# A two-layer vision block: ScalarE's column pieces issued in twos and written in strides, small sums moved to VectorE, other pacing

## The chip, the core and the metric

The kernel runs on one core of a Trainium2 chip. The time is the device time of one execution in microseconds. Three executions of the kernel before took 2607.11, 2608.24 and 2595.48 us; the median is 2607.11. The engines are called TensorE (PE in the profile), VectorE (DVE), ScalarE (ACT), GpSimd (POOL) and SyncE (SP, which here only issues DMAs). All arithmetic is float32.

## What is computed

The input is x, 2 images of 56 x 56 positions with 384 channels. Layer 0 is neighborhood attention and an MLP, layer 1 a convolution with running averages in four directions and an MLP. The part that matters here is layer 1:

```python
h = layernorm(x)
p = h @ w_in + b_in                      # 384 -> 768 channels
local = conv3x3_depthwise(p, k_conv)
lr, rl = ema(local, axis=2), ema(local, axis=2, reverse=True)   # along rows
tb, bt = ema(local, axis=1), ema(local, axis=1, reverse=True)   # along columns
mixed = 0.25 * (lr + rl + tb + bt) + local
x = x + (layernorm(mixed) @ w_out + b_out)
out = x + gelu(layernorm(x) @ w1 + b1) @ w2 + b2
```

with ema: y[t] = 0.6 y[t-1] + 0.4 x[t].

## The kernel before

**Order of the work.** The attention fills the first quarter of the span. Then `passes` runs two loops over groups of up to 512 tokens (four tiles of 128). The first loop (`groups`) does layer 0's MLP for a group and, one group behind, layer 1's input projection `project_in`, which writes p to DRAM. The second loop (`dgroups`) does layer 1's output projection `project_out` and its MLP. In some groups at the start and in the tail of the second loop the matrix products are computed with seven half-size products in place of eight (`hidden_by_seven`, `tokens_by_seven`); they need sums of weight blocks (`sums_of_w1`, `sums_of_w2`) and of input halves (`sums_of_input`, tile `xsums`), made beforehand by GpSimd.

**Work beside TensorE.** The convolution and the scans are VectorE work with channels on the partitions. They are cut into jobs of class `Band` (some rows of one image, one block of 128 channels: eight tap instructions, two row scans) and `Columns` (one image, one block of 128 channels: the two column scans). There are six channel blocks and two images, so 12 `Columns` jobs. Class `Beside` holds the jobs and issues their instructions step by step between the matrix products: each `beside.go(worth)` adds `rate * worth` us to a debt and issues steps until their estimated times have paid it. `MLP`, `OUT` and `ROW` are such worths, 2.6, 3.9 and 7.8. `later(issue, steps)` puts something off by so many steps. `until(name)` issues everything up to a job at once. The order so found is written into the queues of the engines; each engine works through its own queue in order.

**Columns.** A scan along columns needs the image with columns laid out one after another. `turn` (L1342) makes two tiles `line`, one for each half of the columns, from two tiles `loc` (upper and lower rows): four copies of 128 x 392 for each, so eight for a job. `both_ways` (L1245) scans a tile forward and backward, 3.41 us each on VectorE. For image 0 the results go into `mixed` by VectorE (L1386). For image 1 `turn_back` (L1360) makes ScalarE write them into two tiles `mixed`, eight pieces a job (L1366), and `add_to_mix` (L1323) lets a GpSimd DMA accumulate these into `mix_d` in DRAM. The first four copies of a job are issued at the end of the job in front of it (`behind.turn`, L1318 and L1394), the other four at the first step of the job's own first scan (L1376). All copies in the run of the trace were ScalarE's. The copies read 14 columns of 28 rows: the inner loop of the read runs down a column, with a step of 56 elements, and the write is in a row.

**Buffers.** `loc` and a band's input `pt` share two buffers, `line` and a band's `loc` three, `mixed`, `both` and others four. ScalarE also empties TensorE's banks: `hid` (L1206, a hidden tile through gelu, needed every 2.58 us), `mx` (L1501), `hT` (L272, transposed input), the output copies L1882 and L1953, and the seeds L1223, which put a residual into a bank ahead of a token product. Three banks serve the hidden tiles, two the token products.

**Normalization.** In the first loop, `ahead_of` (L1758) normalizes the finished group's tokens in MLP steps 4 to 7 (tile `xn`, L255), stores them at step 8, and transposes them at step 11.

Of the kernel before, what the change touches and what calls it, by code (L numbers as in the profile page):

```python
# [35 lines left out]
ALU = mybir.AluOpType  # L36
# [30 lines left out]
HALF = H // 2  # L67
QUARTER = 14
# [45 lines left out]
class Beside:  # L114
# [3 lines left out]
    def __init__(self):  # L118
        self.jobs, self.due, self.finished, self.idle = [], 0.0, set(), True
        self.late, self.rate = [], 1.0  # L120
        self.steps = self.run()
# [55 lines left out]
def block_kernel(ctx: ExitStack, tc: tile.TileContext, ins: dict, out: bass.AP):  # L177
    nc = tc.nc
# [913 lines left out]
    def passes(xs, xn, w1, w2, between=lambda ps: None):  # L1092
# [164 lines left out]
        class Band:  # L1257
# [31 lines left out]
            def steps(self):  # L1289
                beside.behind(Band)  # L1290
                if self.loc is None:
                    self.centre(nc.vector)
                    yield us(self.n)
                loc, pt = self.loc, self.pt
                for dy in (-1, 0, 1):
                    for dx in (-1, 0, 1):
                        if dy == 0 and dx == 0:
                            continue
                        lo, hi = max(self.lo, -dy), min(self.hi, H - max(0, dy))
                        xs, xt, n = max(0, -dx), max(0, dx), W - abs(dx)  # L1300
# [12 lines left out]
                behind = beside.behind()  # L1313
                yield from both_ways(both, loc)
                if isinstance(behind, Band):
                    behind.centre()
                if isinstance(behind, Columns):
                    behind.turn(nc.scalar.copy)  # L1318
                beside.later(lambda: nc.scalar.mul(flat(both), flat(both), share), 8)  # L1319
                beside.later(lambda: add_to_mix(self.b, self.m, at, both), 11)  # L1320
# [4 lines left out]
        class Columns:  # L1325
# [15 lines left out]

            def turn(self, copy):  # L1342
                c, t = len(self.lines), half("line", "work", 3)
                for i in range(0, HALF, QUARTER):
                    for h in range(2):
                        at = slice(c * HALF + i, c * HALF + i + QUARTER)
                        copy(  # L1347
                            t[:, i : i + QUARTER, h * HALF : (h + 1) * HALF],
                            self.loc[h][:, :, at].rearrange("p h w -> p w h"),
                        )  # L1350
                self.lines.append(t)

            def steps(self):
                if not self.lines:

                    self.turn(nc.gpsimd.tensor_copy)
                    yield 2.5
                mixed, behind = [], None

                def turn_back(c):  # L1360
                    if not mixed:
                        mixed.extend(half("mixed", "out", 4) for h in range(2))
                    for i in range(0, HALF, QUARTER):
                        at = slice(c * HALF + i, c * HALF + i + QUARTER)
                        for h in range(2):
                            nc.scalar.mul(  # L1366
                                mixed[h][:, :, at],
                                self.lines[c][:, i : i + QUARTER, h * HALF : (h + 1) * HALF]
                                .rearrange("p w h -> p h w"), share,
                            )  # L1370

                for c in range(2):
                    t = self.lines[c]
                    for step, took in enumerate(both_ways(t, t)):
                        if c == 0 and step == 0:
                            self.turn(nc.scalar.copy)  # L1376
                            for h in range(2) if self.b == 0 else ():
                                mixed.append(half("mixed", "out", 4))
                                nc.sync.dma_start(out=flat(mixed[h]), in_=self.rows(mix_d, h))
                        yield took  # L1380
                        if step == 0:
                            behind = beside.behind()
                    if self.b == 0:
                        for h in range(2):
                            to = mixed[h][:, :, c * HALF : (c + 1) * HALF]
# [4 lines left out]
                            yield us(HALF / 2, 2.0)  # L1390
                    else:
                        beside.later(lambda c=c: turn_back(c), 1 + c)
                if isinstance(behind, Columns):
# [136 lines left out]

        def sums_of_w1(w1, three):

# [5 lines left out]
            for to, x, y in (  # L1538
                (t1, b12, b11), (t2, b22, t1), (t3, b22, b12), (t4, b21, t2),
                (other, w1[:, 2, :h], w1[:, 2, h:]),  # L1540
            ):
                nc.gpsimd.tensor_tensor(to, x, y, ALU.subtract)
            return t1, t2, t3, t4, other
# [79 lines left out]

        def sums_of_w2(w2):

# [5 lines left out]
            for to, x, y in ((t1, b12, b11), (t2, b22, t1), (t3, b22, b12), (t4, b21, t2)):  # L1631
                steps.append(lambda to=to, x=x, y=y: nc.gpsimd.tensor_tensor(to, x, y, ALU.subtract))
            return (t1, t2, t3, t4), steps
# [97 lines left out]
        for g, (t0, n) in enumerate(groups):  # L1731
# [26 lines left out]
            def ahead_of(m):  # L1758

                nonlocal xn_w, hT_w  # L1760
                if waiting is not None:
                    gw, x2w, norm_w = waiting
                    nw = groups[gw][1]
                    at = 4
                    if m == 1 and gw >= EARLY.stop:
# [6 lines left out]
                    if at <= m < at + nw:  # L1772
                        norm_w.apply_by_scalar(m - at, x2w, xn_w)
                    if m == (9 if g <= EARLY.stop else 8):
                        store_x2(gw, x2w)
# [140 lines left out]
        w2 = w2_1  # L1916
# [4 lines left out]

        hT = channels(first["xn"], dgroups[0][1], *n2)
        for g, (t0, n) in enumerate(dgroups[:switch]):
            hid = []
# [7 lines left out]
            for k in range(n):  # L1932
                if g == switch - 1 and k == 2:
# [4 lines left out]
                    three = wp.tile([P, NC, INNER], F32, name="w1_t", tag="w_in")  # L1938
                    w1_sums = sums_of_w1(w1, three)
                    w2_sums, steps = sums_of_w2(w2)  # L1940
                    for step in steps:
                        step()
                if k == n - 1:
# [18 lines left out]
        ps_m = ps_u  # L1962
        xsums = sums_of_input(hT)
        for g, (t0, n) in enumerate(dgroups):
            if g < switch:
# [135 lines left out]
```

## Time and profile before

| | |
|---|---|
| median of three runs | 2607.11 us |
| the profiled execution's own time | 2604.78 us |
| its span, first to last instruction | 2603.0 us |
| mean granted TensorE clock | 0.993 |
| TensorE busy with matmuls | 2554.5 us, 98% |
| VectorE busy | 1957.9 us, 75% |
| ScalarE busy | 1137.1 us, 44% |
| GpSimd busy | 569.3 us, 22% |
| `line<-loc` (L1347), ScalarE, 96 pieces | 80.3 us |
| `mixed<-line` (L1366), ScalarE, 48 pieces | 40.3 us |
| weight sums of the tail, GpSimd | from 1930.0 to 1949.9 us |

A busy share is the time in which an engine had an instruction running. TensorE's matmuls overlap and their ends are modelled, so its 98% is not a distance to its peak; what counts is where it had to wait. The view of waits lists, for an engine and a line, who ended its idle time, in total, how often, and the longest. The timeline lists instructions in order of time: start, length, engine, line, operation, output and input tiles, and in brackets the idle time ahead of it and what ended that. The windows show busy time and the granted clock of a stretch. In the convolution stage, 900 to 1950 us, the columns of image 0 lie between 1272 and 1532, those of image 1 between 1798 and 1929.

### The profile page before, as it was taken

To read this page: it belongs to the slowest core of one execution; us is meant where nothing else is said; L and a number is where in the kernel's file an instruction comes from. 1 tells how busy PE (TensorE), PEld (TensorE's weight loads), DVE (VectorE), ACT (ScalarE), POOL (GpSimd) and SP (SyncE) were. 2 spreads that over 40 slices of the span, in tenths; PEclk is the share of its full clock that TensorE was granted. 3 is DMA by queue.
4 is the path that set the end of the run, shared out by engine and by line. 5 is a ranking of instruction groups with operands and counts; after the bars stand their busy time and mean duration, and the time that the engine had idled before them with its cause. 6 is when DMAs were issued, how large, how long until landed. Compare 5 with 4: busy or idle time off the path is not lost. (4 is left out here: it accounts for less than half of the span.)

```text
span 2603.0 us, 41611 instructions
## 1 busy us (share of the span) xinstructions
PE 2554.5 (98%) x16438; PEld 1697.8 (65%) x16438; DVE 1957.9 (75%) x3763; ACT 1137.1 (44%) x2043; POOL 569.3 (22%) x619
## 2 busy tenths in 40 slices
PE   9999999999999999999999999999899999999999
PEld 5666666666788644555445545555458888888888
DVE  3888878887444489967789968898767778878771
ACT  4655655655443344433554343334752332333222
POOL 0111111111542011110110101011153333333332
PEclk9999999999999999999999999999999999999999
DMA  6422454225412356555665656776870333333210
GB/s 219 151 95 95 155 182 153 82 95 197 131 43 61 92 157 166 160 143 135 192 218 196 182 161 203 228 201 177 190 194 15 74 73 74 73 73 73 46 28 21
DMA packets 162158, 338.49 MB, mean 130 GB/s; under 512 B 12086, under 2 KB 113952, under 8 KB 159648
## 3 DMA queue, kind: packets, MB, share of 16 engines
q1 hardware_dynamic: 128064, 251.18, 28.5%
q0 software_dynamic: 28944, 57.81, 13.6%
q10 hardware_dynamic: 4944, 26.74, 3.0%
q8 instruction: 131, 2.15, 0.3%
q14 instruction: 75, 0.61, 0.1%
HBM read 171.91 MB, written 134.88 MB: 118 GB/s over the span
## 5 line engine op out<-in xcount | busy, mean ns | idle before, releaser
L1302 DVE SCALAR_TENSOR_TENSOR loc<-pt,taps,loc 128x495 f32<-128x495 f32 (+13 forms) x432 | 397.9, 921 | 49.0 <-ACT loc L1285 35.1
L1195 PE MATMUL mm<-hT,w 128*128 128x512 f32 x864 | 382.3, 597 | 7.0 <-ACT hid L1206 6.4
L1195 PEld LDWEIGHTS mm<-hT,w 128*128 128x128 f32 x864 | 162.5, 191 | 203.2 <-issue 185.6
L571 ACT ACTIVATE pts<-pts 119x448 f32<-119x448 f32 (+5 forms) x396 | 210.8, 573 | 109.3 <-DVE pts L561 104.2
L561 DVE TENSOR_TENSOR pts<-sc,bias 119x448 f32<-119x448 f32 (+5 forms) x396 | 219.2, 616 | 45.9 <-PE sc L550 45.6
L1213 PE MATMUL y_end<-w,hid 128*128 128x384 f32 x648 | 215.2, 489 | 3.7 <-ACT y_end L1223 3.7
L1213 PE MATMUL y<-w,hid 128*128 128x384 f32 x648 | 213.6, 486 | 0.5 <-ACT y L1223 0.5
L1442 DVE STREAM_TRANSPOSE turned<-mx 32x192 f32<-32x192 f32 x528 | 194.9, 369 | 20.6 <-DMA mix_d<-mixed 13.7
L404 PE MATMUL ps<-hT,wqkv 128*128 128x448 f32 x504 | 207.9, 557 | 2.1 <-ACT vs L449 1.5
L1178 DVE STREAM_TRANSPOSE hT<-xn 32x96 f32<-32x96 f32 x656 | 176.8, 269 | 26.0 <-ACT xn L255 17.5
L1195 PE MATMUL mm<-hT,w_in 128*128 128x512 f32 x396 | 174.3, 598 | 8.9 <-ACT mx L1501 6.8
L1213 PEld LDWEIGHTS y_end<-w,hid 128*128 128x128 f32 x648 | 123.5, 191 | 89.4 <-ACT y_end L1223 4.0
L1213 PEld LDWEIGHTS y<-w,hid 128*128 128x128 f32 x648 | 122.3, 190 | 84.5 <-ACT y L1223 1.1
L1206 ACT ACTIVATE hid<-mm,chan 128x512 f32<-128x512 f32 x144 | 98.5, 688 | 180.3 <-PE mm L1195 180.3
L404 PEld LDWEIGHTS ps<-hT,wqkv 128*128 128x128 f32 x504 | 92.5, 192 | 86.2 <-issue 76.1
L1195 PEld LDWEIGHTS mm<-hT,w_in 128*128 128x128 f32 x396 | 75.5, 192 | 105.4 <-issue 88.8
L1323 POOL DMA_DIRECT2D mix_d<-both x54 | 51.0, 944 | 404.3 <-ACT both L1319 219.1
L227 POOL TENSOR_TENSOR rs<-rs,mhalf 128x4 f32<-128x4 f32 (+4 forms) x56 | 55.7, 995 | 320.7 <-DVE rs L224 311.0
L550 PEld LDWEIGHTS sc<-qT,kT 32*100 32x100 f32 (+3 forms) x3168 | 87.8, 169 | 46.4 <-DVE sum L580 7.6
L590 PE MATMUL o<-pts,vt 100*32 100x112 f32 (+3 forms) x3168 | 115.9, 263 | 0.5 <-ACT pts L571 0.5
L1248 DVE TENSOR_TENSOR_SCAN line<-decay,line 128x1568 f32<-128x1568 f32 x24 | 81.9, 3414 | 41.3 <-ACT line L1347 41.3
L620 PE MATMUL ps<-wproj,og 128*128 128x384 f32 x294 | 107.0, 504 | 2.8 <-DVE og L533 2.1
(191 smaller groups left out, 4681.8 us busy)
## 6 DMA issues: line engine op xcount, KB each, us to landing
loc<-loc_d SPq DMA_DIRECT2D x24, 784.0 KB
xa<-x_d SPq DMA_DIRECT2D x24, 768.0 KB
xa<-rows POOLq DMA_DIRECT2D x24, 768.0 KB, 8.2
bias<-in_bias_t ACTq DMA_DIRECT2D x13, 1344.0 KB
p_d<-mx SPq DMA_DIRECT2D x11, 1536.0 KB
mx<-mix_d SPq DMA_DIRECT2D x11, 1536.0 KB
v_d<-vs SPq DMA_DIRECT2D x49, 192.0 KB
xr<-in_x SPq DMA_DIRECT2D x49, 192.0 KB
```

The source lines that it names most:

```text
L404: nc.tensor.matmul(ps, lhsT=wqkv[:, c, m * P : (m + 1) * P], rhs=hT[:, c, half_of(n)], start=c == 0, stop=c == NC - 1,)
L550: nc.tensor.matmul(sc[i // 2][: w.keys, i % 2, q : q + TT], lhsT=kT[d, hg, w.keys_at + r * w.kc : w.keys_at + (r + w.rows) * w.kc], rhs=qT ...
L561: nc.vector.tensor_tensor(self.pts[:n, h : h + 2, lo:hi, :], sc[half][:n, :, at * TT : (at + hi - lo) * TT].rearrange("p h (c q) -> p h c ...
L571: nc.scalar.activation(t, t, AF.Exp)
L590: nc.tensor.matmul(o[i * HD : (i + 1) * HD, self.slot, :TT], lhsT=w.vt[:n, c, h * HD : (h + 1) * HD], rhs=self.pts[:n, i, c, :], start=c = ...
L620: nc.tensor.matmul(ps, lhsT=ogs[t // 7][:, c, at : at + P], rhs=wproj[:, c, :], start=c == 0, stop=c == NC - 1,)
L1178: nc.vector.transpose(hT[j : j + HD, :, k * P + i : k * P + i + HD], xn[i : i + HD, k, :].rearrange("p (c q) -> p c q", c=NC)[:, :, j : j ...
L1195: nc.tensor.matmul(ps[:, : n * P], lhsT=w[:, c, m * P : (m + 1) * P], rhs=hT[:, c, : n * P], start=c == 0, stop=c == NC - 1,)
L1206: nc.scalar.activation(t[:, : n * P], ps[:, : n * P], AF.Gelu, bias=col(b1, m))
L1213: nc.tensor.matmul(ps, lhsT=t[:, k * P : (k + 1) * P], rhs=w[:, m, :], start=m == 0 and onto is None, stop=m == len(lhs) - 1, skip_group_c ...
L1302: nc.vector.scalar_tensor_tensor(to, pt[:, lo + dy - self.top : hi + dy - self.top, xt : xt + n], self.tap(dy, dx), to, ALU.mult, ALU.add,)
L1442: nc.vector.transpose(t[j : j + HD].rearrange("p (m c) -> p m c", m=NI)[:, :, i : i + HD], mx[i : i + HD, :, k * P + j : k * P + j + HD],)
```

## The change

- `turn` and `turn_back` swap loops: a piece now reads along rows (28 rows of 14 columns, or 14 of 28) and writes with a step of 56 elements.
- `turn` can do one half alone. A job's own second `line` is made in twos, two pieces at each of its first tile's two scans. `turn_back` does two pieces at a time, at steps 0 and 1 after a tile is scanned and no longer four at step 1 or 2. A job turned behind another `Columns` still gets its first four pieces in one go.
- A `Columns` job straight after a `Band` is no longer turned by ScalarE at the band's end, but by VectorE at its own start. There are three such jobs, so 12 pieces.
- The next job's load is asked for at the end of the first tile's second scan, and once more a step later.
- `Beside.rate` is 1.06, and 0.98 from the second loop on.
- In the first loop, from the group after `EARLY.stop` on, tokens are normalized in steps 6 to 9 and stored at step 10.
- In front of the tail, VectorE makes the sums of w1 and w2; those of w2 are issued after `sums_of_input`.

```diff
-        self.late, self.rate = [], 1.0
+        self.late, self.rate = [], 1.06
...
                     behind.centre()
-                if isinstance(behind, Columns):
-                    behind.turn(nc.scalar.copy)
...
-            def turn(self, copy):
-                c, t = len(self.lines), half("line", "work", 3)
-                for i in range(0, HALF, QUARTER):
-                    for h in range(2):
+            def turn(self, copy, halves=(0, 1)):
+
+                if halves[0] == 0:
+                    self.lines.append(half("line", "work", 3))
+                c, t = len(self.lines) - 1, self.lines[-1]
+                for h in halves:
+                    for i in range(0, HALF, QUARTER):
                         at = slice(c * HALF + i, c * HALF + i + QUARTER)
                         copy(
-                            t[:, i : i + QUARTER, h * HALF : (h + 1) * HALF],
-                            self.loc[h][:, :, at].rearrange("p h w -> p w h"),
+                            t[:, i : i + QUARTER, h * HALF : (h + 1) * HALF]
+                            .rearrange("p w h -> p h w"),
+                            self.loc[h][:, :, at],
                         )
-                self.lines.append(t)
...
-                    self.turn(nc.gpsimd.tensor_copy)
+                    self.turn(nc.vector.tensor_copy)
...
-                def turn_back(c):
+                def turn_back(c, h):
...
-                        for h in range(2):
-                            nc.scalar.mul(
-                                mixed[h][:, :, at],
-                                self.lines[c][:, i : i + QUARTER, h * HALF : (h + 1) * HALF]
-                                .rearrange("p w h -> p h w"), share,
-                            )
+                        nc.scalar.mul(
+                            mixed[h][:, :, at].rearrange("p h w -> p w h"),
+                            self.lines[c][:, i : i + QUARTER, h * HALF : (h + 1) * HALF], share,
+                        )
...
+                        if c == 0:
+                            self.turn(nc.scalar.copy, (step,))
                         if c == 0 and step == 0:
-                            self.turn(nc.scalar.copy)
...
-                        if step == 0:
+                        if c == 0 and step == 1 or c == 1 and step == 0:
                             behind = beside.behind()
...
-                        beside.later(lambda c=c: turn_back(c), 1 + c)
+                            beside.later(lambda c=c, h=h: turn_back(c, h), h)
...
-                    at = 4
+                    at = 4 if g <= EARLY.stop else 6
...
-                    if m == (9 if g <= EARLY.stop else 8):
+                    if m == (9 if g <= EARLY.stop else 10):
                         store_x2(gw, x2w)
...
+        beside.rate = 0.98
         for g, (t0, n) in enumerate(dgroups[:switch]):
...
-                    w1_sums = sums_of_w1(w1, three)
-                    w2_sums, steps = sums_of_w2(w2)
-                    for step in steps:
-                        step()
+                    w1_sums = sums_of_w1(w1, three, nc.vector)
+                    w2_sums, sum_steps = sums_of_w2(w2, nc.vector)
...
         xsums = sums_of_input(hT)
+        for step in sum_steps:
+            step()
```

More of the change, by code (lines that the diff above doesn't have):

```diff
@@ L1380, in steps @@
                         yield took
-                        if step == 0:
+                        if c == 0 and step == 1 or c == 1 and step == 0:
                             behind = beside.behind()
-                    if self.b == 0:
-                        for h in range(2):
+                    for h in range(2):
+                        if self.b == 0:
                             to = mixed[h][:, :, c * HALF : (c + 1) * HALF]
@@ L1390, in steps @@
                             yield us(HALF / 2, 2.0)
-                    else:
-                        beside.later(lambda c=c: turn_back(c), 1 + c)
+                        else:
+                            beside.later(lambda c=c, h=h: turn_back(c, h), h)
                 if isinstance(behind, Columns):
@@ L1529, in measure_by_steps, with sums_of_w1 @@
                 yield from measure_by_vector(ahead[0], ahead[2], k)
-        def sums_of_w1(w1, three):
+        def sums_of_w1(w1, three, engine=nc.gpsimd):
             h = HID // 2
@@ L1541, in sums_of_w1 @@
             ):
-                nc.gpsimd.tensor_tensor(to, x, y, ALU.subtract)
+                engine.tensor_tensor(to, x, y, ALU.subtract)
             return t1, t2, t3, t4, other
@@ L1622, in hidden_by_seven, with sums_of_w2 @@
             return low, high, lambda: finish(2)
-        def sums_of_w2(w2):
+        def sums_of_w2(w2, engine=nc.gpsimd):
             q = NHID // 2
@@ L1631, in sums_of_w2 @@
             for to, x, y in ((t1, b12, b11), (t2, b22, t1), (t3, b22, b12), (t4, b21, t2)):
-                steps.append(lambda to=to, x=x, y=y: nc.gpsimd.tensor_tensor(to, x, y, ALU.subtract))
+                steps.append(lambda to=to, x=x, y=y: engine.tensor_tensor(to, x, y, ALU.subtract))
             return (t1, t2, t3, t4), steps
```

## The prediction

> **What bounds the kernel now.** I read the busy times first, then TensorE's waits between 880 and 1975 us (the convolution stage and the hand-over to the tail), then the timeline of TensorE around each long wait, and last ScalarE's, VectorE's and GpSimd's timelines at the same moments. The columns of a wait are total us, times, longest.
>
> ```profile
> PE 2554.5 (98%) x16438; PEld 1697.8 (65%) x16438; DVE 1957.9 (75%) x3763; ACT 1137.1 (44%) x2043; POOL 569.3 (22%) x619
> ...
> PE mm L1195 <- ACT mx L1501: 6.8, 2, 6.0
> PE mm L1195 <- ACT hid L1206: 6.4, 4, 3.6
> PE uz L1574 <- POOL xsums L1555: 5.5, 1, 5.5
> PE y_end L1213 <- ACT y_end L1223: 3.7, 1, 3.7
> PE mm L1195 <- ACT hT L272: 2.2, 2, 1.6
> ```
>
> TensorE sets the time; only what makes it wait counts. The waits of this stage are few and long. The timeline gives place and cause (start, length, the wait in brackets):
>
> ```profile
> 1285.47 4.60 PE L1195 MATMUL mm<-hT,w_in 128*128 128x512 f32 x6 [5.96 <-ACT mx L1501]
> ...
> 1279.06 5.78 ACT L1347 COPY line<-loc 128x392 f32<-128x392 f32 x7 [5.73 <-DMA loc<-loc_d]
> ...
> 1844.72 9.70 PE L1213 MATMUL y_end<-w,hid 128*128 128x384 f32 x24 [3.74 <-ACT y_end L1223]
> ...
> 1841.27 2.52 ACT L1366 ACTIVATE mixed<-line 128x392 f32<-128x392 f32 x3 [9.47 <-DMA mix_d<-mixed]
> ...
> 1950.68 2.07 PE L1574 MATMUL uz<-xsums,w_t 128*128 128x256 f32 x4 [5.53 <-POOL xsums L1555]
> ...
> 1949.90 0.73 POOL L1555 TENSOR_TENSOR xsums<-hT 128x256 f32<-128x256 f32 x1
> ```
>
> So ScalarE, which empties TensorE's banks, is itself held in its queue: at 1273 by a column piece whose input is still on its way, at 1832 by a piece whose output buffer still feeds a DMA. At 1950 GpSimd comes to xsums only after nine weight sums.
>
> A wait also costs what follows it. The six matmuls at 1285.47 took 4.60 us where six took 2.74 at 1263.90: 1.86 more. The windows say why: granted clock 0.86 in 1275 to 1300, 1.00 beside it. In the same way the 24 at 1844.72 took 9.70 and not 7.90 (1.80), the twelve after a 3.61 us wait at 1870.14 took 8.38 and not 5.32 (3.06), and the first eight at 1950.68 took 3.98 and not 2.06 (1.92). The two short waits at 1515.10 (1.69) and 1519.54 (1.60) cost nothing after them.
>
> [...]
>
> ```profile
> L1347 ACT COPY line<-loc 128x392 f32<-128x392 f32 x96 | 80.3, 921 | 8.4 <-DMA loc<-loc_d 8.4
> L1366 ACT ACTIVATE mixed<-line 128x392 f32<-128x392 f32 x48 | 40.3, 915 | 17.4 <-DMA mix_d<-mixed 9.5 <-issue 4.7 <-DVE line L1252 1.7
> L1319 ACT ACTIVATE both<-both 128x504 f32<-128x504 f32 x24 | 14.8, 616 | 7.2 <-DVE both L1252 7.2
> ```
>
> A row of 504 takes 616 ns, a strided read of 392 takes 921. [...]
>
> **Part 1: pieces read in a row, written in strides.** 84 of 96 line pieces and all 48 back pieces stay on ScalarE. Lower end of a piece: the row price, 616 - 112 x 0.837 = 522 ns (0.837 is the slope between the 504 and 1008 rows, 616 and 1038). Upper end, if a strided write pays as a strided read: 921. The only strided write of weight in the trace is L1250, in place with step 56: 178 ns for the small ones, 213 for 28 elements, some 35 ns for 18 to 19 more, read and write together. That is no more than VectorE's strided read alone (L1386: 784 in 1616 ns), so I exclude far more than 921 but can't tell the two apart. I take 550 ns, about 430 back to back (the overlap of the old ones is 921 against 835).
>
> **Part 2: the first column of a run by VectorE.** Three columns per run come straight after a band, so twelve pieces go to VectorE[...]. At 1273.8 VectorE stood idle 7.82 us anyway, waiting for ScalarE's pieces, which waited for the same DMA. The wait moves to a queue nobody needs in these 8 us; ScalarE no longer stands, TensorE no longer stalls. What is queued behind on VectorE are scans and norms used many steps later. Gain: 5.96 + 1.86 = 7.8. The second such place is 1505 to 1512: ScalarE waits 2.65 us for loc, does seven pieces in 5.90, and TensorE loses 1.69 + 1.60 = 3.3. In the built order only two plus two pieces stand there, between hidden tiles. Gain 3.3. If VectorE's wait were not covered, norms would come up to 8 us late; the cover is the five or six hidden steps of 2.58 us (13 to 15 us) between the statistics and their use. The next column's load on SP's queue is now asked for one scan later, 3.4 us; in part 4 it lands before its pieces' turn all the same.
>
> **Part 3: weight sums by VectorE.** Nine sums leave GpSimd (5 x 1.81 + 4 x 2.62 = 19.5 us, from 1930.0 to 1949.9). [...] It ended its last scan at 1925.7 and idled 13.72 us until 1939.4[...]. [...] GpSimd can start xsums when hT is there, 1937.3, and needs four of 0.73: ready at 1940.2, before TensorE asks at 1945.1. Gain 5.53 + 1.92 = 7.5. What is late next: nothing that the trace shows up to 1959. [...]
>
> **Part 4: image 1's columns, 1785 to 1930.** In the built order a column's pieces stand as 6 + 2, 2 + 2, 2, 2 instead of 8, 8. Before, this stretch cost 3.74 + 1.80 and 0.89 + 3.61 + 3.06 = 13.1 us. The first of these is not removed. The second column's second back piece still writes into the buffer of the first column's first half (same address as before), and that is free only when the accumulate DMA has landed: 10.8 us after its issue (1830.47 to 1841.27). GpSimd issues it behind the row add L1134, which waits for the four xn at about 1829, so it lands near 1841 again. ScalarE is now held with ten pieces ahead of the seed that TensorE needs at 1840.6: 1841.3 + 10 x 0.43 + 0.9 = 1846.5. That is a wait of 6 to 6.5 us and 2 of slow clock, 8.5. After it, with short pieces, the hidden tiles at 1862 to 1870 are emptied in time: 0 for 7.6. Net gain 4.6.
>
> **Part 5: paces and later xn.** 1.06 instead of 1.0 issues side work 6% earlier; image 1's first column starts some 11 us earlier in the built order, and 0.98 after that lets the end fall at the same token tile as before. VectorE is busy 88% of 1550 to 1700, so it can follow. Normalizing from step 6 puts xn beside the next group's xn in steps 8 and 9: two xn of 0.62, a hidden 0.6 and a centre 0.7 in 2.58 us still fit. One new burst, six pieces before the last hidden tile and two before hT near 1340, costs 0.5 at 430 ns a piece. The store of x2 moves from step 8 to 10 on SP's queue, ahead of nothing that needs it: dgroups read it hundreds of us later; 0. All else 0, between -2 and +12 (rival C).
>
> **Sum**, against the profiled execution (span 2603.0, its own time 2604.8): -7.8 - 3.3 - 7.5 - 4.6 + 0.5 = -22.7, so 2582. That run lies 2.3 below the median of 2607.1; for a median I forecast 2607.1 - 22.7 = 2584.4, rounded 2585.
>
> **Rivals.** A: the above, chance 0.50. B: the strided write pays like the strided read, 921 ns. Then part 4 gives 10 x 0.835 for 4.3 in the held queue, some 10.5 + 2.5 of stall and 1.5 later, 14.5 for 13.1, and the burst near 1340 costs 3.8 + 1.5: -18.6 + 1.4 + 5.3 = -12, 2595. For it: the reads pay[...]. Chance 0.26. C: the pace overfills VectorE, which is at 95% in 975 to 1100, norms come late and TensorE waits for hT some 2 us in each of six groups, +12: 2597. Against it: xn moved two steps later leaves 5 us more. Chance 0.14. D, slower: a strided write dearer than a strided read. ScalarE has 92 pieces and about 27 us of other work in the 140 us of part 4, some 15 of them held by DMA: from (140 - 15 - 27)/92 = 1.07 us a piece it sets the pace there, and from 1.27 it has eaten the 18.6. At 1.45 it costs 35: 2623. L1250 speaks against it. Chance 0.06. That nothing changes in the stages is left 0.04.
>
> **Chances and range.** About 0.5% (13 us) is what a measurement tells from no change: faster means under 2594. Nine tenths of A, half of B, a third of C: 0.64. Slower is D and a little of C, 0.08; the rest, 0.28, the same. The range goes from A with part 4 fully gained (-31.2, 2576) to C with a late drain, 2603.
>
> **What would show it.** L1348 and L1366 on ScalarE near 550 ns (A) or 920 (B). No wait of TensorE by L1501 near 1280 and none by xsums near 1945; a VectorE piece waiting for loc in its place. A wait by the seed near 1840, longer than 3.74. I am wrong if TensorE's waits by hT grow in the groups before 1700, or if a stall as long as the removed ones stands elsewhere.

## The result and the profile after

| | before | after |
|---|---|---|
| median of nine runs | 2605.09 us | 2589.35 us |
| lowest to highest | 2595.48 to 2608.24 | 2583.09 to 2594.36 |
| the profiled execution's own time | 2604.78 | 2583.09 |
| its span | 2603.0 | 2581.3 |

The ratio is 0.9945, 95% interval 0.993 to 0.9961: 15.7 us (of medians) faster. The forecast was 2585; its sum of -22.7 is 7 us more than the 15.7 that came.

The two spans differ by 21.7, and not all of that is the change's. A fixed point helps: the priming matmul `yb<-zeros` (L1227) stands once in front of layer 0's MLP and once in front of the tail. Up to the first one the code is the same in all kernels of this study, yet it starts at 671.28 us before, at 663.78 after, and in the twelve experiments between 664.6 and 674.3. So 7.5 of the 21.7 lie in a stretch that the change doesn't touch. From here on I compare two lengths: the **middle**, first priming to second, and the **tail**, second priming to the end of the span.

| | middle | tail | sum |
|---|---|---|---|
| before | 1272.2 | 659.5 | 1931.7 |
| after | 1265.3 | 652.2 | 1917.5 |

That makes -6.9 and -7.3, together -14.2. The medians give 15.7, and the ratio of 0.9945 stands for 14.3.

Where TensorE waits now, in 880 to 1975 us; first the view of waits after (engine, line, by whom: total us, times, longest):

```profile
PE y_end L1213 <- ACT y_end L1223: 11.5, 1, 11.5
PE mm L1195 <- ACT hT L272: 3.6, 2, 2.9
PE y L1213 <- DVE xc L1471: 1.9, 1, 1.9
PE mm L1195 <- ACT hid L1206: 0.3, 1, 0.3
```

Against the list of before, `mx` (6.8) and `xsums` (5.5) are gone and `hid` is down from 6.4 to 0.3; the seed has grown from 3.7 to 11.5. The timeline of TensorE after gives the places:

```profile
1341.87 17.41 PE L1195 MATMUL mm<-hT,w_in 128*128 128x512 f32 x36 [2.91 <-ACT hT L272]
1642.27 5.83 PE L1213 MATMUL y<-w_out,mx 128*128 128x384 f32 x12 [1.86 <-DVE xc L1471]
1837.51 9.72 PE L1213 MATMUL y_end<-w,hid 128*128 128x384 f32 x24 [11.46 <-ACT y_end L1223]
1929.11 0.33 PE L1227 MATMUL yb<-zeros 128*128 128x384 bf16 x1
```

Each wait again has its slow clock behind it: 36 matmuls took 17.41 where 36 take 15.72 elsewhere (1.69), twelve 5.83 where twelve after the same wait took 4.14 in other runs (1.69), 24 took 9.72 and not 7.90 (1.82). The windows show a granted clock of 0.91 in 1341 to 1360, 0.79 in 1642 to 1650 and 0.82 in 1837 to 1848, and 1.00 in 1300 to 1340.

The pieces, forms kept apart, after:

```profile
L1348 ACT COPY line<-loc 128x392 f32<-128x392 f32 x84 | 65.7, 938 | 1.8 <-DMA loc<-loc_d 1.8
L1366 ACT ACTIVATE mixed<-line 128x392 f32<-128x392 f32 x48 | 39.6, 950 | 23.5 <-DMA mix_d<-mixed 12.3 <-issue 5.7 <-DVE line L1252 5.6
```

One piece takes 938 or 950 ns, not 550. Back to back it is less: 65.7 us over 84 is 0.78 a piece, where 80.3 over 96 was 0.84. In the queue near 1830 ten pieces take 7.18 us, 0.72 each, where eight took 6.66 before, 0.83 each. And VectorE's new work, its timeline after:

```profile
1261.90 0.98 DVE L1348 COPY line<-loc 128x392 f32<-128x392 f32 x2
1263.94 0.90 DVE L1348 COPY line<-loc 128x392 f32<-128x392 f32 x2 [1.05 <-DMA loc<-loc_d]
...
1908.79 0.93 DVE L1542 TENSOR_TENSOR w_t<-w 128x768 f32<-128x768 f32 x1
...
1913.24 1.35 DVE L1632 TENSOR_TENSOR w_t<-w 128x1152 f32<-128x1152 f32 x1
```

The sums took 0.93 to 0.96 us (128x768) and 1.35 to 1.36 (128x1152). They end at 1918.5, before `hT` is there. The first pieces wait only 1.05 us for `loc`, where ScalarE had waited 5.73. That is the first surprise: something other than the choice of engine has made that load early.

### The profile page after: what moved, and what is told of

Read it like the earlier page. It is cut to its first block, busy times and chain, and to the rows that moved or that the text cites. A ratio compares the mean times of both kernels' runs of the same rounds, so it can differ in the third digit from the quotient of the medians.

```text
span 2581.3 us, 41602 instructions
## 1 busy us (share of the span) xinstructions
PE 2541.9 (98%) x16436; PEld 1692.9 (66%) x16438; DVE 1973.0 (76%) x3785; ACT 1116.9 (43%) x2030; POOL 559.7 (22%) x610
## 3 DMA queue, kind: packets, MB, share of 16 engines
q0 software_dynamic: 28944, 57.81, 13.6%
## 5 line engine op out<-in xcount | busy, mean ns | idle before, releaser
L1213 PE MATMUL y_end<-w,hid 128*128 128x384 f32 x648 | 215.2, 489 | 11.5 <-ACT y_end L1223 11.5
L1442 DVE STREAM_TRANSPOSE turned<-mx 32x192 f32<-32x192 f32 x528 | 194.8, 369 | 11.1 <-issue 4.2
L550 PE MATMUL sc<-qT,kT 32*100 32x112 f32 (+3 forms) x3168 | 106.5, 268 | 3.7 <-DVE pts L561 3.7
```

Of the source, the lines that this page charges most:

```text
L550: nc.tensor.matmul(sc[i // 2][: w.keys, i % 2, q : q + TT], lhsT=kT[d, hg, w.keys_at + r * w.kc : w.keys_at + (r + w.rows) * w.kc], rhs=qT ...
L1213: nc.tensor.matmul(ps, lhsT=t[:, k * P : (k + 1) * P], rhs=w[:, m, :], start=m == 0 and onto is None, stop=m == len(lhs) - 1, skip_group_c ...
L1442: nc.vector.transpose(t[j : j + HD].rearrange("p (m c) -> p m c", m=NI)[:, :, i : i + HD], mx[i : i + HD, :, k * P + j : k * P + j + HD],)
```

## The experiments

All times are medians; every ratio is to the kernel before on the same chip, with its 95% interval. Middle and tail are from the profiled execution of each.

| kernel | us | ratio | middle | tail |
|---|---|---|---|---|
| after | 2589.35 | 0.9945 [0.993, 0.9961] | 1265.3 | 652.2 |
| e1 after, strided reads | 2590.28 | 0.9938 [0.9925, 0.9951] | 1268.3 | 652.2 |
| e2 after, sums on GpSimd | 2592.11 | 0.9945 [0.9932, 0.9958] | 1262.2 | 656.4 |
| e3 after, first pieces on ScalarE | 2591.29 | 0.9947 [0.9934, 0.9959] | 1265.3 | 651.8 |
| e4 after, row add late | 2572.54 | 0.9878 [0.9861, 0.9894] | 1249.7 | 652.2 |
| e5 after, old paces | 2591.11 | 0.9947 [0.9933, 0.996] | 1261.8 | 656.8 |
| e6 e5 and first pieces on ScalarE | 2593.88 | 0.9957 [0.9943, 0.9972] | 1271.7 | 651.8 |
| e7 before, new paces | 2592.78 | 0.9952 [0.9938, 0.9967] | 1262.4 | 659.4 |
| e9 after, xn early | 2587.82 | 0.9935 [0.9919, 0.9951] | 1265.1 | 652.2 |
| e10 e4, turn split | 2577.06 | 0.9898 [0.9879, 0.9918] | 1253.4 | 651.9 |
| e12 e4, old pieces | 2574.19 | 0.9879 [0.986, 0.9898] | 1250.4 | 652.2 |
| b2 before, first pieces on VectorE | 2593.82 | 0.9959 [0.9944, 0.9974] | 1261.5 | 661.6 |
| b3 before, sums on VectorE | 2595.10 | 0.9969 [0.9961, 0.9977] | 1273.3 | 651.8 |

The whole times of e1, e2, e3, e5, e6, e7, e9 and b2 are not told apart from after's; what the variants of the changed kernel show is in the waits of their traces, one trace each. e7, b2 and b3 are told apart from the kernel before: on the same chip 2604.39 became 2592.78, 2604.79 became 2593.82, and 2604.79 became 2595.10.

### Who removed the waits near 1285 and 1515: VectorE's pieces or the pace?

The theory of the prediction is the engine: a wait on VectorE's queue holds nobody. The rival is the pace, which the prediction had put at 0.

**e3.** Part 2 of the change undone:

```diff
                 if isinstance(behind, Band):
                     behind.centre()
+                if isinstance(behind, Columns):
+                    behind.turn(nc.scalar.copy)
```

> The changed kernel with the first four pieces of a run of columns on ScalarE at the end of the band ahead of it again, as before (12 pieces). Theory (ScalarE stands in its queue behind pieces whose input is not there yet): TensorE's waits near 1275 and 1510 come back, some 8 and 3 us with the slow clock after the first, 8 to 11 us slower, 2597 to 2600. Rival (the twos and the earlier load have taken the wait away on their own): within 2 us of the changed kernel.

Neither wait came back. ScalarE's timeline in e3 shows the pieces in the old place, and next to no wait for the load:

```profile
1264.69 1.62 ACT L1350 COPY line<-loc 128x392 f32<-128x392 f32 x2
1266.53 3.09 ACT L1350 COPY line<-loc 128x392 f32<-128x392 f32 x4 [0.22 <-DMA loc<-loc_d]
```

So in the changed kernel the choice of engine is worth nothing there. In 1800 to 1930 the waits stand differently (3.38, 3.45 and 3.52 in place of one of 11.46); the middle is the same, 1265.3.

**e5, e6, e7.** The pace, with and without part 2. e5 is after, e6 is e3, with

```diff
-        self.late, self.rate = [], 1.06
+        self.late, self.rate = [], 1.0
...
-        beside.rate = 0.98
```

and e7 is the kernel before with the two new rates and nothing else.

> The changed kernel with the old pace, 1.0 in both loops; VectorE's pieces, the twos, the sums and the later xn stay. Theory P (it is the pace that took ScalarE's wait near 1275 away: at 1.06 the band ahead of the column ends some 4 us earlier against TensorE, its buffer comes free earlier and the column's load lands before the pieces' turn): VectorE now waits 5 to 8 us for loc near 1280, but TensorE still does not, since VectorE's pieces hold nobody; within 3 us of the changed kernel up to 1800, and the wait by the seed near 1840 may move. Theory V (it is VectorE's pieces alone, the pace is nothing): the same here; the next kernel tells them apart.

> The changed kernel with the old pace and with the first pieces of a run on ScalarE at the end of the band. Theory P (pace and VectorE's pieces each cover the same wait): with both covers gone, TensorE's wait by mx near 1280 is back, 4 to 6 us and up to 1.9 of slow clock, and 1.5 to 3.3 near 1515; 5 to 9 us slower than the kernel with the old pace alone. Rival (the later xn or the pieces in twos took it away): no wait over 2 us near 1280, within 2 us.

> The kernel before with the new paces alone, 1.06 and then 0.98. Theory P: the waits near 1285 (5.96 and 1.86 of slow clock) and near 1515 (1.69 and 1.60) shrink to 2 us or less in all, 8 to 11 us faster than the kernel before if the columns of image 1 and the tail lose nothing, about 2596. Rival (the wait needs VectorE's pieces or the later xn to go): both waits stay, within 3 us of the kernel before.

In e5 TensorE has no wait over 0.55 us before 1640. Its tail, though, is 4.6 longer than after's: at the old pace the last columns end later, ScalarE stands 5.00 us in the tail until an accumulate DMA has landed, and TensorE 2.76 with 1.8 of slow clock after it. In e6 the waits are back, here the first and the second pair on TensorE's timeline:

```profile
1276.11 4.54 PE L1195 MATMUL mm<-hT,w_in 128*128 128x512 f32 x6 [3.22 <-ACT mx L1503]
1503.41 1.20 PE L269 MATMUL tp<-ident,xn 128*128 128x128 f32 x9 [1.85 <-ACT xn L255]
1508.25 15.72 PE L1195 MATMUL mm<-hT,w_in 128*128 128x512 f32 x36 [1.07 <-ACT hT L272]
```

With 1.8 of slow clock (4.54 for 2.74) that is 7.9 us, and the middle of e6 is 9.9 longer than that of e5. So the middle of the changed kernel is 1271.7 with neither (e6), 1261.8 with the engine alone (e5), 1265.3 with the pace alone (e3) and 1265.3 with both: either one, engine or pace, is enough, and the second adds nothing.

On the kernel before, e7 has the pace alone. TensorE's timeline shows what is left of the wait near 1285, and a new one:

```profile
1271.49 5.42 PE L1195 MATMUL mm<-hT,w_in 128*128 128x512 f32 x12 [1.25 <-ACT mx L1501]
...
1344.22 17.41 PE L1195 MATMUL mm<-hT,w_in 128*128 128x512 f32 x36 [2.83 <-ACT hT L272]
```

Of the three waits of 5.96, 1.69 and 1.60 and the 1.86 of slow clock, 1.25 and 1.58 are left, 8.3 us less. The expectation had 2 or less in all. The middle is 9.8 shorter, but that is a sum of several things: image 1's stretch costs about 9 where it cost 13.1, and the wait near 1344 is new, 2.83 with 1.69 of slow clock, though the pieces are the old ones. It is not in e5, which has the new pieces at the old pace. So the burst near 1340, eight pieces in a row ahead of `hT`, comes with the pace.

Why a pace does it shows in ScalarE's timeline of e7:

```profile
1263.14 0.90 ACT L1347 COPY line<-loc 128x392 f32<-128x392 f32 x1
1265.01 5.84 ACT L1347 COPY line<-loc 128x392 f32<-128x392 f32 x7 [0.97 <-DMA loc<-loc_d]
```

Before, the same seven stood 5.73 us. SyncE's timeline has the two `loc` DMAs, merged into one line, before and then in e7:

```profile
1261.52 9.97 SPq L1340 DMA_DIRECT2D loc<-loc_d  x2
```

```profile
1253.94 6.67 SPq L1340 DMA_DIRECT2D loc<-loc_d  x2
```

Counted from the first priming, the second of SyncE's two `loc` DMAs went out at 600.2 before (1271.5) and at 595.8 in e7 (1260.6): 4.4 earlier. It went out 0.4 us after VectorE's last tap of the band ahead (1271.1 and 1260.2), whose input shares the two buffers with `loc`; so it is the band that set it, and at the new pace VectorE does that band earlier. And it landed faster, in 4.4 us and not 7.6. The DMA queues of the two stretches suggest why. First before, 1271.5 to 1279 us (packets, MB, share of the 16 engines), then e7, 1260.6 to 1265:

```profile
q0 software_dynamic: 526, 0.83, 76.4%
q1 hardware_dynamic: 169, 0.96, 32.7%
```

```profile
q1 hardware_dynamic: 206, 1.19, 83.2%
```

Queue 0 has GpSimd's DMAs (in before they add up to 57.8 MB, and its profile gives queue 0 57.81), and what was in it before is the row add `xa<-rows` (L1134, an accumulate DMA that adds a bias row to a group's residual, issued at 1268.80) and a `both`. In e7 nothing of queue 0 moves in that stretch, though the row add is issued at 1261.74; in before the load shares the engines with it. No run moves that row add alone, so this part is not shown. As measured, a load that is asked for 4.4 us earlier came 7.5 us earlier against TensorE's work.

**b2.** The prediction's part 2 by itself, on the kernel before: the band's end no longer turns, and the column's start uses VectorE.

```diff
-                if isinstance(behind, Columns):
-                    behind.turn(nc.scalar.copy)
...
-                    self.turn(nc.gpsimd.tensor_copy)
+                    self.turn(nc.vector.tensor_copy)
```

> The kernel before with the first four pieces of a run of columns on VectorE at the column's start, and nothing else of the change. Theory (a wait on VectorE's queue holds nobody, on ScalarE's it holds TensorE's banks; either this or the pace is enough): the waits near 1285 and 1515 go, 5.96, 1.86, 1.69 and 1.60 us, 8 to 11 us faster than the kernel before, 2594 to 2598. Rival (at the old pace VectorE, held by the load, falls behind, and norms or the columns of image 1 give it back): at most 4 us faster.

The three waits and the slow clock after the first are gone, 0.80 near 1331 is the only wait of over 0.55 before 1640: the 11.1 us of the prediction. ScalarE, though, still waits. VectorE's and then ScalarE's timeline of b2:

```profile
1277.85 1.39 DVE L1345 COPY line<-loc 128x392 f32<-128x392 f32 x3 [5.48 <-DMA loc<-loc_d]
```

```profile
1277.85 2.60 ACT L1345 COPY line<-loc 128x392 f32<-128x392 f32 x3 [3.78 <-DMA loc<-loc_d]
```

ScalarE's own four pieces come one bank later in its queue, so it is held for 3.78 and then busy for 2.60 us, 6.4 in all and not 11.5, and TensorE, with three banks, shows no wait there. The middle falls by 10.7. Near 1836 the wait by the seed grows to 9.13 (3.74 before), `hid` falls, and the tail's wait by `xsums` is 7.86.

### The weight sums

**b3** is the kernel before with part 3 alone, **e2** the changed kernel without it:

```diff
-                    w1_sums = sums_of_w1(w1, three, nc.vector)
-                    w2_sums, sum_steps = sums_of_w2(w2, nc.vector)
+                    w1_sums = sums_of_w1(w1, three)
+                    w2_sums, sum_steps = sums_of_w2(w2)
+                    while sum_steps:
+                        sum_steps.pop(0)()
```

> The kernel before with the nine weight sums on VectorE, and nothing else. Theory (as the prediction had it): the wait by xsums of 5.53 and the 1.92 of slow clock after it go, nothing comes in their place, 7.5 us faster, about 2598; up to the tail the trace is that of the kernel before. Rival (the wait turns into one for VectorE's last scans or for hT): 4 us or less.

> The changed kernel with the nine sums of weight blocks on GpSimd again, ahead of xsums as before. Theory (they hold xsums up): GpSimd can start them at about 1913, when the last two accumulate DMAs are issued, and needs 19.9 us, so the first xsums is there at 1933.7 where TensorE asks at 1930.6: a wait of 3 to 4 us and 1.9 of slow clock after it, 5 to 6 us slower, about 2595; a little less than the 7.5 of the kernel before, because the columns end some 1.7 us earlier ahead of the tail. Rival (GpSimd finds room for them, the gain came from elsewhere): within 1 us of the changed kernel.

b3's tail is 7.7 shorter, its middle 1.1 longer. Its TensorE goes on without a wait; the same place in e2 waits. TensorE's timeline, b3 and then e2:

```profile
1941.85 1.03 PE L1574 MATMUL ua<-hT,w 128*128 128x256 f32 x4
1942.71 1.03 PE L1574 MATMUL uz<-xsums,w_t 128*128 128x256 f32 x4
```

```profile
1940.78 1.69 PE L1574 MATMUL uz<-xsums,w_t 128*128 128x256 f32 x4 [2.75 <-POOL xsums L1555]
1942.26 1.91 PE L1574 MATMUL ub<-xsums,w_t 128*128 128x256 f32 x4
```

In e2 the wait is 2.75 (3 to 4 were expected) and the next 16 matmuls lose 1.8 us to the clock (1.69, 1.91, 2.22 for 1.03, 1.10, 1.89); the tail is 4.2 longer than after's. The same edit is worth 7.7 on the kernel before and 4.2 on the changed one, and e2's whole time doesn't show even that: its middle came 3.1 shorter, mostly because the clock stayed up after the waits near 1352 and 1651 (15.72 and 4.14, in after 17.41 and 5.83).

### The later xn

**e9**: steps 4 to 7 and the store at step 8 again.

```diff
-                    at = 4 if g <= EARLY.stop else 6
+                    at = 4
...
-                    if m == (9 if g <= EARLY.stop else 10):
+                    if m == (9 if g <= EARLY.stop else 8):
```

> The changed kernel with the tokens normalized in steps 4 to 7 and stored at step 8 throughout, as before. Theory (as the prediction had it: the later xn is worth nothing, it only gives the statistics time): within 2 us of the changed kernel, the waits by hT unchanged. Rival (statistics come late at 1.06, so xn in step 4 makes ScalarE wait in its queue): waits of 1 to 3 us by hid or hT in several groups before 1700, 5 us slower or more.

The middle is 1265.1 for 1265.3, with the same waits at the same places (2.91, 1.85, 0.65, 11.51). The later xn is worth nothing that shows, as forecast.

### The strides

**e1**: ScalarE's pieces read in strides and write in a row again; VectorE's pieces and everything else are the changed kernel's.

```diff
-                            t[:, i : i + QUARTER, h * HALF : (h + 1) * HALF]
-                            .rearrange("p w h -> p h w"),
-                            self.loc[h][:, :, at],
+                            t[:, i : i + QUARTER, h * HALF : (h + 1) * HALF],
+                            self.loc[h][:, :, at].rearrange("p h w -> p w h"),
...
-                            mixed[h][:, :, at].rearrange("p h w -> p w h"),
-                            self.lines[c][:, i : i + QUARTER, h * HALF : (h + 1) * HALF], share,
+                            mixed[h][:, :, at],
+                            self.lines[c][:, i : i + QUARTER, h * HALF : (h + 1) * HALF]
+                            .rearrange("p w h -> p h w"), share,
```

> The changed kernel with ScalarE's 132 pieces read in strides and written in a row again, as before; the order, the twos and VectorE's 12 pieces stay. Theory (the write in strides costs what the read in strides cost, and saves a little only back to back, 0.72 for 0.83 us a piece): the pieces come out at 915 to 921 ns, the burst near 1340 of eight pieces and the held queue near 1840 of some ten each lose about 1 us more, total 1 to 3 us slower than the changed kernel, 2591 to 2592. Rival (the direction of the stride is where much of the gain comes from): 6 us slower or more, above 2595.

The groups of e1, forms kept apart:

```profile
L1355 ACT COPY line<-loc 128x392 f32<-128x392 f32 x84 | 71.3, 920 | 2.0 <-DMA loc<-loc_d 2.0
L1372 ACT ACTIVATE mixed<-line 128x392 f32<-128x392 f32 x48 | 41.4, 921 | 22.0 <-DMA mix_d<-mixed 12.3 <-issue 5.4 <-DVE line L1252 4.3
```

A piece by itself is 2% to 3% shorter with the stride on the read, but 84 of them keep ScalarE busy for 71.3 us and not 65.7, 0.85 a piece for 0.78. Only the bursts feel it: the wait near 1345 is 3.74 for 2.91, the one near 1840 12.45 for 11.46 with 2.75 of slow clock for 1.82, together 2.75 of the 3.0 us by which the middle is longer. The 0.9 of slow clock is no part of it that can be relied on: e9, with the stride on the write, has 10.59 for the 9.72 of after. So the direction of the stride was worth about 2 us in the waits of this kernel, which its whole time doesn't show.

### The wait of 11.5 us by the seed

ScalarE's timeline after: it stands for 12.28 us because a buffer still feeds an accumulate DMA, and it has ten pieces and an output copy to do before the seed.

```profile
1829.23 1.65 ACT L1366 ACTIVATE mixed<-line 128x392 f32<-128x392 f32 x2 [12.28 <-DMA mix_d<-mixed]
1830.67 4.50 ACT L1348 COPY line<-loc 128x392 f32<-128x392 f32 x6
1834.96 1.66 ACT L1366 ACTIVATE mixed<-line 128x392 f32<-128x392 f32 x2
...
1836.97 0.48 ACT L1223 COPY y_end<-xc 128x384 f32<-128x384 f32 x1
```

GpSimd's timeline after: that DMA goes out behind the row add, which has waited 9.04 us for the normalized tiles.

```profile
1816.84 1.36 POOL L1134 DMA_DIRECT2D xc<-rows  x1 [9.04 <-ACT xn L255]
1817.66 2.36 POOL L1321 DMA_DIRECT2D mix_d<-mixed  x2
```

The pieces that fill the buffers had ended at 1800 and 1806. Before, the DMA went out at 1830.47, when GpSimd had waited 0.95 us for these pieces, so there the row add did not hold up its issue.

What fills the buffers earlier is the pace and not the twos. Counted from the start of the group's first token product with `hid`, the second buffer is full at 4.4 us in after (1801.35), at about 14.3 before (1816.18), at 4.7 with the old pieces at the new pace (e12, 1808.65), and only at about 17 with the twos at the old pace (e5, 1801.61). In e3 and e7 the accumulate DMA happens to stand ahead of the row add in GpSimd's queue (1807.17 and 1819.42 in e3, 1811.02 and 1824.24 in e7), and there no wait by the seed is over 3.4.

**e4**: the row add is issued one token tile later. Its result is the next group's residual, used after twelve hidden tiles of 2.58 us.

```diff
                 if k == n - 3:
                     xn = normalized(norm, x3, dgroups[g + 1][1])
-                    add_row(x3, dgroups[g + 1][1], "b2_1")
                 beside.go(ROW)
+                if k == n - 2:
+                    add_row(x3, dgroups[g + 1][1], "b2_1")
```

> The changed kernel with the row add of the MLP's residual (L1134, a GpSimd DMA that waits for the four normalized tiles) issued one token tile later, so that a column's accumulate DMA no longer stands behind it on GpSimd's queue. Theory (this queue is what holds the DMA, the DMA holds a buffer, the buffer ScalarE, and ScalarE the seed): the accumulate DMA goes out near 1808 and not at 1817.7, lands near 1819 and not 1829, and of TensorE's wait of 11.5 us near 1837 no more than 2 stay, with the 1.8 of slow clock gone: 10 to 12 us faster, 2577 to 2580. Rival (the DMA is late for another reason, or ScalarE's ten pieces alone are enough to keep the seed back): the wait stays at 6 us or more, at most 5 us faster.

GpSimd, ScalarE and TensorE in e4, at the same place:

```profile
1809.33 1.82 POOL L1321 DMA_DIRECT2D mix_d<-mixed  x2
...
1819.65 1.49 POOL L1134 DMA_DIRECT2D xc<-rows  x1
```

```profile
1818.44 1.66 ACT L1366 ACTIVATE mixed<-line 128x392 f32<-128x392 f32 x2
1819.89 4.55 ACT L1348 COPY line<-loc 128x392 f32<-128x392 f32 x6
```

```profile
1827.45 7.91 PE L1213 MATMUL y_end<-w,hid 128*128 128x384 f32 x24
1844.53 2.84 PE L1195 MATMUL mm<-hT,w 128*128 128x512 f32 x6 [1.45 <-ACT hid L1206]
```

The wait is gone entirely, and its slow clock too. The middle is 15.6 shorter than after's: 11.46 + 1.82 + 0.30 less 1.45, which is 12.1 for this place, and 3.4 because the clock stayed up after the two shorter waits, which no run ties to the row add. This is a version that beats both kernels: 2572.54, ratio 0.9878 [0.9861, 0.9894].

**e12**: e4 with ScalarE's pieces as they were before, in eights and fours, read in strides, and the next job's load asked for as before; paces, VectorE's pieces (here read in strides too), sums and later xn stay.

> The kernel with the late row add (2572.5) with ScalarE's pieces as they were before: eight in a go, four back pieces at a time and one or two steps later, read in strides; paces, VectorE's pieces and sums, late xn and the late row add stay. Theory (the twos are worth a few us in the stretch of image 1, once the row add no longer spoils it; the strides about 3): waits of 5 to 8 us between 1800 and 1880 against 1.5 there, 5 to 10 us slower than the late row add, 2578 to 2583. Rival (the headline of the change, the pieces, is worth nothing): within 2 us of 2572.5.

The rival holds. GpSimd, ScalarE and TensorE in e12:

```profile
1815.06 1.82 POOL L1321 DMA_DIRECT2D mix_d<-mixed  x2
```

```profile
1821.91 2.57 ACT L1364 ACTIVATE mixed<-line 128x392 f32<-128x392 f32 x3 [0.40 <-DMA mix_d<-mixed]
1824.39 6.66 ACT L1345 COPY line<-loc 128x392 f32<-128x392 f32 x8
```

```profile
1833.18 7.91 PE L1213 MATMUL y_end<-w,hid 128*128 128x384 f32 x24
```

With the DMA out at 1815.06, ScalarE waits only 0.40 us for the buffer, though its pieces stand in eights, and TensorE has no wait over 0.55 between 1680 and 1922. The burst near 1351 costs 3.76 where e4 has 2.92. The middle is 0.7 longer, the ratio the same (0.9879 and 0.9878). The rebuilt pieces, by strides and twos, are worth nothing that can be measured once the row add is out of the way. No run has the old pieces in the changed kernel with the row add where it was.

**e10**: e4 with the next job's four pieces cut in two and two, to break the burst near 1342.

```diff
+                        if c == 1 and step == 1 and isinstance(behind, Columns):
+                            behind.turn(nc.scalar.copy, (0,))
...
-                    behind.turn(nc.scalar.copy)
+                    behind.turn(nc.scalar.copy, (0, 1) if not behind.lines else (1,))
```

> The kernel with the late row add, and the four pieces for the next columns job cut in two and two, the first two at the second scan of the job in front. Theory (near 1342 six pieces stand in a row ahead of the last hidden tile, and that is TensorE's wait of 2.9 us by hT and now and then 1.7 of slow clock): with two and four it drops to 1 us or less, 2 to 4 us faster, 2569 to 2571. Rival (the two earlier pieces wait for their load and hold ScalarE there): a new wait of 2 us or more, the same or slower.

The wait by `hT` falls from 2.92 to 1.47, where the theory had 1 or less, and the rival comes true near 1850. ScalarE's and TensorE's timeline in e10:

```profile
1840.37 1.64 ACT L1348 COPY line<-loc 128x392 f32<-128x392 f32 x2 [4.22 <-DMA loc<-loc_d]
```

```profile
1850.47 4.26 PE L1195 MATMUL mm<-hT,w 128*128 128x512 f32 x6 [5.36 <-ACT hid L1206]
```

The earlier pieces reach ScalarE before their load has landed, and hold it: the same fault as the one near 1285 of the kernel before. The middle is 3.7 longer than e4's.

## Why the prediction was right in the sum and wrong in its parts

- **Part 2, forecast 7.8 + 3.3:** the size is right. By itself, on the kernel before, it takes away all the waits that it was to take (b2, middle -10.7). The picture was half right: ScalarE still waits for the load in b2 (3.78), it only has four pieces fewer behind that wait. What was missed is that the pace takes 8.3 of the 11.1 away on its own (e7), so that in the changed kernel part 2 adds nothing (e3). The forecast counted part 2 and put the pace at 0; that the sum came out the same, since two causes shared one gain, is luck.
- **Part 3, forecast 7.5:** right, in size and cause. b3 measured 7.7 in the tail, and before and after differ there by 7.3. Nothing came in the place of the wait.
- **Part 1, forecast 550 ns:** wrong. A piece takes 938 to 950 ns, the upper bound that was rival B's. The step that failed is "the lower end of a piece: the row price"; reading in a row gave nothing: with the stride on the write a piece takes no less than the 915 to 921 ns that it took with the stride on the read. Only back to back is it cheaper, by some 0.1 us (0.72 for 0.83, where 0.43 was forecast), and e1 puts that at about 2 us of waits.
- **Part 4, forecast 8.5 for 13.1:** the chain was right in every link (row add, accumulate DMA, buffer, ten pieces, seed), the size was rival B's: 11.46 + 1.82 + 0.30 = 13.6, where B had 14.5 and A 8.5. So the net gain of 4.6 was none. Two terms of the wait were mis-sized. Ten pieces, output copy and seed were to take 5.2 us after the DMA's landing and took 8.2 (1829.23 to 1837.45). And the DMA was to land 0.7 after TensorE asks for the seed (1841.3 and 1840.6), but it landed 3.2 after (1829.23 and 1826.05). So the sign of being wrong that the prediction named, a stall as long as the removed ones elsewhere, did come, at the place where a shorter one was foreseen. It was also taken as given that the DMA has to land so late; e4 shows that this was a matter of one place in GpSimd's queue, worth 12.1 us.
- **Part 5, forecast 0 and 0.5:** the step that failed is the pace at 0. Alone it is worth as much as part 2 alone (0.9952 and 0.9959). The new burst near 1340 cost 2.91 + 1.69 and not 0.5, near B's price (3.8 + 1.5). The later xn is 0 (e9). The store and the pace did no harm (rival C): waits by `hT` grew at that one place only.
- **Rivals C and D** did not come. B was right on the price of the pieces and came out at 2595, A at 2585; 2589 lies between. A sum from the waits that are listed gives -11.1 (part 2 or pace), -7.3 (part 3), +0.5 (part 4), +3.8 (burst near 1340, less the 0.81 near 1363 before), +2.1 (the wait near 1640 and its clock): -12.0. Middle and tail give -14.2. The 2.2 that remain lie in waits too short to be listed or in the clock, and no run here separates them.

So the forecast time was near for a mixed reason: two large steps were right, and the ones that failed, +5.1 in part 4 and +4.1 near 1340, were about a fifth of the sum each; that the pace stood in for part 2 did not show in the sum. Where the gain of the pieces went is settled in the main: the strides had little to give, and with the row add out of the way eights do as well as twos (e12). What the earlier columns of image 1 could have brought, buffers filled some 10 us earlier against TensorE's work by the pace, was held up in GpSimd's queue by a row add.

## What to carry to other kernels

Two edits that each remove the same wait are not to be added, and which of them works is seen only when each is tried alone and each is undone: here the pace and the engine each gave about 11 us to the kernel before, and in the changed kernel the one adds nothing to the other. When a DMA lands late, read the queue of the engine that issues it before the engine that waits: one issue that waits for other data, placed a tile earlier than needed, cost 12 us. Ask what stands in ScalarE's queue ahead of its input, and what stands behind it: before, ScalarE was held for 11.5 us near 1273, by the wait of 5.73 and the 5.78 of its pieces, and TensorE lost 5.96; in b2 it was held for 6.4 and TensorE lost nothing.

## What the runs showed of the hardware

- A piece of 128x392 takes ScalarE about the same with a stride of 56 float32 elements on the write (938 to 950 ns in after and e4) as on the read (915 to 926 in before, e1, e7 and e12). No run copies 392 elements without a stride on either side; the 522 ns for such a row are the prediction's estimate from the rows of 504 and 1008 (616 and 1038 ns in before). Back to back the stride on the write is the cheaper one: 0.78 us of busy time a piece (65.7 over 84) against 0.85 (71.3 over 84 in e1).
- VectorE does the same strided write in 0.51 to 0.61 us a piece (after, twelve pieces).
- A short wait sometimes costs a slow clock and sometimes not: after the same wait of 2.9 us by `hT`, 36 matmuls took 17.41 us in after and e9, and 15.72 in e2 and e4. After one of 1.84 to 1.86 us, twelve took 5.83 in after and e1 and 4.14 in e2, e3, e4, e7, e9, e10 and e12. Nothing in these traces says which it will be, so each such case is 1.7 us of chance in a comparison.
- Of two accumulate DMAs of tiles `mixed` (784 KB each), the first freed its buffer 10.8 and 11.6 us after the issue when a row add of 768 KB was issued just ahead (before, 1830.47 to 1841.27; after, 1817.66 to 1829.23), and 6.9 us after it when the row add followed later (e12, 1815.06 to 1821.91).
